# Checking equal entries in a graph kernel: a compare on the transposed blocks replaced by one on natural rows that TensorE adds up

## The chip, the cores and the metric

The kernel runs on one core of a Trainium2 chip. The time is the device time of one launch in microseconds (us), as the median of several runs on the same chip. The engines are TensorE (PE in the profile), VectorE (DVE), ScalarE (ACT), GpSimd (POOL) and SyncE (SP), which here issues most of the transfers. Each engine works through its own instructions in order and waits for the others by semaphores. Data lies in DRAM, in SBUF, and in PSUM, which has eight banks and takes TensorE's sums.

## The reference, cut to what matters

There are 2708 nodes with 128 features each (`x`) and an adjacency matrix `adj` of 2708 x 2708 floats. The matrix is sparse; every row has its diagonal set and is divided by its number of entries, so all nonzero entries of row i are equal to 1/degree(i).

```python
# adj: random pattern OR identity, then each row divided by its sum
# layer 0
XW = mobius_matvec(W, X)
gamma = 2.0 / jnp.maximum(1.0 - sq, EPS)               # sq = row sums of XW * XW
nominator = A_hat @ (gamma * XW)
denominator = _clamp_abs(A_hat @ (gamma - 1.0))
m = mobius_scalar_mul(0.5, nominator / denominator)
r = A_hat.sum(-1, keepdims=True)
AXW = mobius_scalar_mul(r, m)
x = _layernorm(x + expmap0(relu(logmap0(AXW))))
# layer 1
s = x @ msg_w[:, :D].T ;  d = x @ msg_w[:, D:].T
messages = gelu(s[:, None, :] + d[None, :, :] + msg_b)   # for every pair i, j
aggregated = jnp.einsum('ijd,ij->id', messages, adj)
new_feats = concat([x, aggregated]) @ upd_w.T + upd_b
x = _layernorm(x + layernorm(gelu(new_feats) + x))
```

## The kernel before, in words

**Sparsity and its check.** The kernel does not multiply by the values of `adj`, but by its pattern, and it evaluates messages for the entries that are set only. This holds if the nonzero entries of a row all equal the row's diagonal entry. The kernel counts the nonzero entries (`nn`) and the entries that equal the diagonal (`ne`); at the end a `verdict` (lines 1442 to 1476) compares the sums of the two and a few other conditions, and its flag decides whether a general path runs as well (`tc.If(dense > 0)`). With these inputs it does not.

**Layer 0, per block.** `adj` is handed over transposed, in 22 blocks of Q = 124 rows. A block b comes in two halves, each a load of 682 KB into one of three buffers `aT` (line 635), 124 partitions x 1364 floats. For each half ACT takes the sign (line 645) into a bf16 tile `sgn` and counts the entries by its accumulator. Then DVE compares the half with the diagonal (line 655), which a second small load `dgb` (line 631, 62 KB, the diagonal of the block on all partitions) has brought:

```python
V.scalar_tensor_tensor(aT, aT, 1.0, diagonal broadcast to [Q, HALF, Q],
                       op0=OP.mult, op1=OP.is_equal, accum_out=ne[:, at : at + 1])
```

The buffer is held by the load, the sign and the compare. TensorE multiplies `sgn` with `ym`, the features in three bf16 limbs and some columns of powers of two (line 670). DVE adds the limbs up (`total`, line 700) and reads from the further columns, in digits, which neighbours a row has (lines 720 and 722); ACT takes the squares and the relu.

**From sums to messages.** `batch` turns the digits of some blocks into neighbour lists: index lists `J`, and one-hot matrices `R` (line 903), for tiles of up to 128 edges. One of its steps multiplies on TensorE into a PSUM bank `sel` (line 916), and DVE finds the place of each edge in it (`nearest`, lines 921 to 931). `epilogue` does the rest of layer 0 for a chunk of blocks (0-4, 5-8, 9-13, 14-18, 19-21). `project` then stores one row of message terms per node in a table in DRAM (line 1136): table 0 for blocks 0 to 8, table 1 for blocks 9 to 21 (`CUT` = 9). `messages` works on groups of up to four tiles: POOL gathers the rows of the neighbours from a table (line 359, one gather per tile, five buffers `dd` of four tiles), TensorE spreads the terms of the receiving node (`X`, line 1189) and transposes `R` into the PSUM bank `rt` (line 1192), ACT copies that out (`turned`, line 1196), DVE adds (line 1200), ACT takes the gelu (line 1204), and TensorE collects the sums (lines 1211 to 1214). 66 tiles need table 0 only, the other 41 need table 1. `ended` and `finish` make the outputs, 22 stores.

**The order of the work.** All of it is written down as steps with a cost, the buffers that they hold (`Slot`, with the counts in `ROOM`) and a rank. A list scheduler, `Plan.order`, simulates the engines with these costs: whatever can start first is issued, and the rank decides among steps that could start within 0.04 us. So the program of each engine, SP's queue included, is a fixed order. The steps of layer 0 have the block's number as their rank, the compares b + 0.6, an epilogue the number of its chunk's end less `AHEAD`, the messages ranks from 23 (table 0) and from 40 (table 1), and the verdict 29.

Of the kernel before, what the change touches and what calls it, by code (L numbers as in the profile page):

```python
# [10 lines left out]
F32 = mybir.dt.float32  # L11
U32 = mybir.dt.uint32
BF16 = mybir.dt.bfloat16
I32 = mybir.dt.int32
AF = mybir.ActivationFunctionType
OP = mybir.AluOpType
AX = mybir.AxisListType

P = 128
Q = 124  # L20
NB = 22
NP = NB * Q
HALF = NB // 2
# [12 lines left out]
CUT = 9  # L36
# [13 lines left out]
BEHIND = 8.0  # L50
AHEAD = 1.0
SPARE = [("R", 44), ("R", 85), ("sl", 22), ("sl", 44)]
LIFT = (0.0, 0.0, 20.0, 20.0, 0.0)
PACES = (23.0, 0.1), (40.0, 0.4)
BEGUN = dict(PE=0.9, ACT=3.5, DVE=0.9, POOL=20.0, SP=3.0)
LANDED = (1.8, 3.8, 5.8, 7.8)
ENGINES = {getattr(mybir.EngineType, e) for e in ("PE", "DVE", "Activation", "Pool", "SP")}
ROOM = dict(
    op=2, sel=1, X=3, Xm=2, rt=1, ag=1, aT=3, dgb=2, sgn=2, v=2, front=1, back=2, cols=1,
    x1T=2, d=2, stmp=2, st=5, near=1, r0=2, dd=DDS, rw=2, ge=2, agT=4, fin=3,  # L60
)
ENDS = [4, 4, 4, 3, 3, 2, 1, 1]
LATE_ORDER = [9, 10, 11, 12, 13, 14, 15, 16, 17, 18, 8, 7, 0, 6, 5, 1, 4, 19, 3, 20, 2, 21]


# [92 lines left out]
def hyperbolic_then_message_kernel(  # L158
# [8 lines left out]
    adj_t: bass.AP,  # L167
    adj_r: bass.AP,
    w0: bass.AP,
# [9 lines left out]
    nc = tc.nc  # L179
    N, D = x.shape  # L180
# [44 lines left out]
    rowvec = dict(mbr=weights[:, 4 * D : 5 * D], ub=weights[:, 5 * D :])  # L225
    keep_c = const.tile([P, 2 * D + 1 + NB], F32, name="keep_c")
    nc.scalar.dma_start(keep_c, c_l)
    rowvec["lw"], rowvec["lb"] = keep_c[:, :D], keep_c[:, D : 2 * D]
    mb, dg = keep_c[:, 2 * D : 2 * D + 1], keep_c[:Q, 2 * D + 1 :]

# [10 lines left out]
    ones = const.tile([P, P], F32, name="ones")  # L241
    nc.gpsimd.memset(ones, 1.0)

    def power(o, v, k):
# [4 lines left out]
    for c in range(NB):  # L249
# [8 lines left out]
        compare_op=OP.is_equal,  # L258
# [39 lines left out]
    nn = const.tile([Q, 2 * NB], F32, name="nn")  # L298
    ne = const.tile([Q, 2 * NB], F32, name="ne")
    mv = const.tile([Q, NB, 2], F32, name="mv")  # L300
# [37 lines left out]

    def bank(name, bufs=2):
        return ps.tile([P, 512], F32, name=name, bufs=bufs)  # L340

    nc.gpsimd.memset(bias, 0.0)
# [278 lines left out]
    def layer0(b):  # L621

        dgs, ops = Slot("dgb"), Slot("op")
        home = SPARE[b - 2] if 2 <= b < 2 + len(SPARE) else None
        sgs = [] if home else [Slot("sgn")]
        st = {}
        rank = float(b)

        def diagonal():
            st["dgb"] = dgb = stream.tile([P, Q], F32, name="dgb", bufs=2)  # L630
            nc.sync.dma_start(dgb, bass.AP(tensor=adj_r.tensor, offset=adj_r.offset + b * Q, ap=[[0, P], [1, Q]]))

# [18 lines left out]

        def compare(h):
            aT = st[h][:Q]
            at = 2 * b + h
            V.scalar_tensor_tensor(  # L655
                aT,
                aT,
                1.0,
                st["dgb"][:Q].unsqueeze(1).to_broadcast([Q, HALF, Q]),
                op0=OP.mult,  # L660
                op1=OP.is_equal,
                accum_out=ne[:, at : at + 1],
            )

        def product(j0, j1):
# [7 lines left out]

        ld = add("SP", 0.38, diagonal, holds=[dgs], rank=rank, kb=62.0)
        p = None
        for h in range(2):
            ats = Slot("aT")
            la = add("SP", 0.46, lambda h=h: load(h), holds=[ats], rank=rank + 0.1 * h, kb=682.0)
            g = add("ACT", 1.33, lambda h=h: sign(h), after=[la], holds=[ats, *sgs], rank=rank)
            compared.append(add("DVE", 1.5, lambda h=h: compare(h), after=[g, ld], holds=[ats, dgs], rank=rank + 0.6))  # L680
            for j in (0, 6):
                j0, j1 = h * HALF + j, h * HALF + (6 if j == 0 else HALF)
                p = add(
                    "PE",
                    0.218 * (j1 - j0),
                    lambda j0=j0, j1=j1: product(j0, j1),
                    after=[g, p, limbed[(j1 - 1) // 4]],
                    holds=[*sgs, ops],
                    rank=rank + 0.5,
                )  # L690
# [46 lines left out]
        if not S:  # L737
            found[b] = counted[b]
        squared[b] = add("ACT", 1.08, squares, after=[summed[b]], rank=rank + 0.7)

    def batch(blocks, S, rank):
# [176 lines left out]
        def nearest(k, part, s):  # L918
            w, ta = len(part), part[0][0]
            dist = row.tile([P, 512], F32, name="dist", bufs=1)[:, : w * C].rearrange("p (t c) -> p t c", c=C)  # L920
            V.tensor_tensor(  # L921
                dist, s["sp"], place[:, ta : ta + w].unsqueeze(2).to_broadcast([P, w, C]), op=OP.subtract
            )
            yield
            near = row.tile([P, 64], F32, name="near", bufs=1)[:, :w]
            V.tensor_reduce(near, dist, axis=AX.X, op=OP.min, apply_absolute_value=True)
            yield
            if k == 0:
                V.tensor_scalar_min(J[:, ta : ta + w], near, lim[0] - 1.0)
            else:  # L930
                V.tensor_scalar(J[:, ta : ta + w], near, -float(lim[0]), lim[1] - 1.0, op0=OP.add, op1=OP.min)

        for k in range(2):
            every = []
            late = rank + 0.5 + k * BEHIND
            for i in range(n):
# [9 lines left out]
                for t in range(t0, t0 + nt):  # L946
                    hot[t] = oh
                    every.append((t, i))
            for g in range(0, len(every), 512 // C):
                part = every[g : g + 512 // C]  # L950
                w = len(part)
# [216 lines left out]
    def messages(k, blocks, rank, pace, ended):  # L1168
# [15 lines left out]
        def spread(st, group):  # L1184
            st["X"] = X = bank("X", ROOM["X"])
            st["RT"] = RT = ps.tile([P, 4, P], BF16, name="rt", bufs=1)
            for i, (t, b, *_) in enumerate(group):
# [6 lines left out]
        def turned(st, w):  # L1194
            st["rw"] = rw = edge.tile([P, 4, Q], F32, name="rw")
            A.copy(rw[:, :w, :], st["RT"][:, :w, :Q])  # L1196

# [180 lines left out]
    for b in range(NB):  # L1378
        layer0(b)
    for blocks, S in BATCHES:  # L1380
        batch(blocks, S, blocks[-1] + 1.5)
    for b0, b1 in CHUNKS:
        epilogue(b0, b1, b1 - AHEAD)

# [62 lines left out]
    def verdict2():  # L1447
# [6 lines left out]
        V.tensor_reduce(cn[:, 1:2], nn, axis=AX.X, op=OP.add)  # L1454
        V.tensor_reduce(cn[:, 2:3], ne, axis=AX.X, op=OP.add)
        V.tensor_reduce(cn[:, 3:4], deg, axis=AX.X, op=OP.add)
# [9 lines left out]
    def verdict5():  # L1466
        tot, bad = vd["tot"], vd["bad"]
        pads = float(NP - N)
        V.tensor_scalar(bad[:, 1:2], tot[:, 0:1], pads, None, op0=OP.not_equal)
        V.tensor_scalar_add(tot[:, 2:3], tot[:, 2:3], -pads * NP)  # L1470
        V.tensor_tensor(bad[:, 2:3], tot[:, 2:3], tot[:, 1:2], op=OP.not_equal)
# [92 lines left out]
def layouts(x, adj, msg_w, msg_b, upd_w, upd_b, ln_w, ln_b):  # L1564
# [10 lines left out]
    diagonal = np.zeros((P, NB), adj.dtype)  # L1575
    diagonal[:Q] = np.diagonal(whole).reshape(NB, Q).T
    return {
        "x_p": x_p,
        "x_t": xs.T,
        "w_l": np.concatenate([msg_w, upd_w, *(np.tile(v, (P, 1)) for v in (msg_b, upd_b))], axis=1),  # L1580
        "c_l": np.concatenate([*(np.tile(v, (P, 1)) for v in (ln_w, ln_b)), msg_b[:, None], diagonal], axis=1),
        "adj_t": adj_t,
        "adj_r": np.diagonal(whole).reshape(NB, Q),
    }
# [37 lines left out]
```

## Time and profile before

| What | Value |
|---|---|
| median of three runs | 371.06 us (369.29 to 371.99) |
| the profiled execution | 424.92 us |
| span of the profile | 422.8 us |
| mean granted TensorE clock in it | 0.808 |
| busy: PE / DVE / ACT / POOL | 270.7 / 282.2 / 236.4 / 166.3 us |
| 44 loads of `aT` | 682 KB each |
| 22 loads of `dgb`, 22 stores to the tables | 62 KB each |
| all DMA | 45.86 MB |
| first gather / last store of table 1 issued | 179.8 us / 313.2 us after the start of the span |

The profile is one execution, slower than the runs. Its page lists for each line of the kernel the operation, the tiles (output <- inputs), their shape, the number of instructions and their summed and mean time, and last how long the engine had been idle before them and what ended most of that. The table of windows gives for stretches of the span the busy time of the engines, in the order PE, weight loads of PE, DVE, ACT, POOL, with the number of instructions in brackets, and then the mean clock, the share of DMA and its GB/s. The chain that ended last runs back from the last instruction, at each step to whatever released it; "issue" is time in which the engine waited for nothing that the profile shows.

### The profile page before, as it was taken

Reading aid. Unit: us, or ns where it says so; the run is one execution under the profiler, and the core shown is the slowest. Engines: PE = TensorE matmul, PEld = TensorE weight load, DVE = VectorE, ACT = ScalarE, POOL = GpSimd, SP = SyncE. Lnnn points to the kernel's source line nnn. Section 1 sums busy time; section 2 is a strip of 40 time slices with the busy share of each in tenths; the row PEclk is TensorE's granted clock in tenths of the full one; section 3 lists DMA queues with packets and bytes.
Section 4 is the critical chain, followed back from the end, with each engine's and each line's share of the span. In section 5 each row is a group of like instructions: output and inputs, shape, how many; then the busy total and the mean of one; then the engine's idle time right before and its main releaser. Section 6 shows DMA issues by size and latency. Waiting matters only on the chain.

```text
span 422.8 us, 6335 instructions
## 1 busy us (share of the span) xinstructions
PE 270.7 (64%) x1769; PEld 193.0 (46%) x1769; DVE 282.2 (67%) x1224; ACT 236.4 (56%) x660; POOL 166.3 (39%) x298
## 2 busy tenths in 40 slices
PE   5300957999763888966877379854863388575720
PEld 5200534665421446644634146553653278564610
DVE  1888967799978999964986079843632028944580
ACT  2858846358885389682667076952651146543430
POOL 9940000010300001076567606782537522877240
PEclk9855698999896999997889569975997589856565
DMA  8678376207340474844247502220112200222110
GB/s 317 233 224 249 125 221 206 71 2 211 110 118 9 139 224 143 271 119 119 21 140 237 126 0 85 66 55 25 29 42 51 48 20 6 54 72 67 32 36 14
DMA packets 19601, 45.86 MB, mean 108 GB/s; under 512 B 5881, under 2 KB 11573, under 8 KB 19557
## 3 DMA queue, kind: packets, MB, share of 16 engines
q1 hardware_dynamic: 15701, 37.75, 29.4%
q0 software_dynamic: 3424, 7.02, 6.9%
q10 hardware_dynamic: 432, 0.60, 0.4%
q8 instruction: 16, 0.26, 0.3%
q14 instruction: 28, 0.23, 0.2%
HBM read 42.58 MB, written 2.78 MB: 107 GB/s over the span
## 4 chain that ended last, share of the span: by engine, by line
PE 25%; DVE 24%; ACT 14%; DMA 13%; another core or an unknown queue 10%; issue 9%; POOL 1%; ACTq 0%; SPq 0%; POOLq 0%; DVEq 0%
DMA aT<-in_adj_t_dram 11%; PE op L670 8%; DVE aT L655 5%; PE X L1189 3%; PE op L1214 3%; ACT sgn L645 2%; PE ag L1214 2%; ACT r L899 2%; PE X L1127 2%; ACT ge L1204 1%; DVE nom L543 1%; PE X L1408 1%; PE ag L1211 1%; PE rt L1192 1%
## 5 line engine op out<-in xcount | busy, mean ns | idle before, releaser
L359 POOL DMA_INDIRECT dd<-table_dram,J x107 | 112.6, 1052 | 53.6 <-issue 42.4
L670 PE MATMUL op<-ym,sgn 124*124 124x512 bf16 x396 | 104.8, 413 | 43.4 <-DVE ym L559 24.5
L670 PEld LDWEIGHTS <-sgn 124*124 124x124 bf16 x396 | 55.0, 147 | 74.1 <-DVE ym L559 24.8
L655 DVE SCALAR_TENSOR_TENSOR aT<-aT,dgb 124x1364 f32<-124x1364 f32 x44 | 69.0, 1572 | 8.7 <-ACT sgn L645 4.1
L645 ACT ACTIVATE sgn<-aT 124x1364 bf16<-124x1364 uint32 x36 | 48.2, 1340 | 12.9 <-DMA aT<-in_adj_t_dram 12.8
L979 POOL TENSOR_TENSOR knr<-knr,halves 124x10 f32<-124x10 f32 (+2 forms) x5 | 9.0, 1810 | 84.4 <-DVE knr L983 84.4
L1189 PE MATMUL X<-sl,R 124*128 124x128 bf16 x321 | 36.1, 251 | 6.7 <-issue 5.6
L1200 DVE TENSOR_TENSOR dd<-X,dd 128x512 f32<-128x512 f32 (+2 forms) x28 | 18.5, 660 | 31.7 <-remote 19.6
L1189 PEld LDWEIGHTS <-R 124*128 124x128 bf16 x321 | 29.0, 115 | 18.1 <-issue 17.0
L246 POOL TENSOR_TENSOR krs<-krs,halves 124x5 f32<-124x5 f32 (+2 forms) x5 | 5.5, 1094 | 79.6 <-DVE krs L1068 74.3
L1192 PE MATMUL rt<-identb,R 124*128 124x124 bf16 x107 | 26.7, 250 | 6.8 <-ACT rw L1196 6.6
L1204 ACT ACTIVATE ge<-dd 128x512 f32<-128x512 f32 (+2 forms) x28 | 17.2, 614 | 16.3 <-remote 6.2
L1214 PE MATMUL ag<-rw,ge 128*128 128x124 f32 x132 | 24.7, 319 | 2.3 <-ACT ge L1204 1.7
L1127 PE MATMUL X<-wall,x1T 128*124 128x512 f32 x38 | 21.4, 644 | 7.5 <-ACT x1T L1123 5.1
L921 DVE TENSOR_TENSOR dist<-sel,place 128x440 f32<-128x440 f32 (+11 forms) x17 | 6.4, 379 | 28.2 <-remote 26.1
L899 ACT ACTIVATE r<-iota,mid 124x256 f32<-124x256 f32 (+4 forms) x48 | 24.6, 534 | 0.4
L246 POOL TENSOR_TENSOR rs<-rs,halves 124x4 f32<-124x4 f32 (+3 forms) x16 | 13.6, 855 | 27.7 <-DVE rs L1270 23.7
L1214 PEld LDWEIGHTS ag<-rw,ge 128*128 128x128 f32 x132 | 21.7, 232 | 3.4 <-ACT ge L1204 2.0
L1211 PE MATMUL ag<-ident,gd 124*128 124x124 f32 x44 | 11.6, 351 | 18.1 <-issue 14.0
L705 ACT COPY cnt<-op 124x1 f32<-124x1 f32 x22 | 3.4, 153 | 32.9 <-remote 18.1
L1214 PE MATMUL op<-rw,ge 128*128 128x124 f32 x82 | 18.6, 359 | 4.9 <-ACT ge L1204 3.7
L1386 ACT COPY gd<-ag 128x124 f32<-128x124 f32 x22 | 5.8, 264 | 26.5 <-remote 21.5
(257 smaller groups left out, 666.5 us busy)
## 6 DMA issues: line engine op xcount, KB each, us to landing
aT<-in_adj_t_dram SPq DMA_DIRECT2D x44, 682.0 KB
dd<-table_dram,J POOLq DMA_INDIRECT x107
x_sb<-in_x_p_dram SPq DMA_DIRECT2D x2, 704.0 KB
own<-in_x_t_dram SPq DMA_DIRECT2D x2, 682.0 KB
dgb<-in_adj_r_dram SPq DMA_DIRECT2D x22, 62.0 KB
table_dram<-d SPq DMA_DIRECT2D x22, 62.0 KB
out_dram<-own SPq DMA_DIRECT2D x21, 62.0 KB
sl<-in_w_l_dram ACTq DMA_DIRECT2D x1, 384.0 KB
```

The costliest lines, as they stand in the source:

```text
L246: nc.gpsimd.tensor_tensor(o, v, halves[:Q, k : k + 1].to_broadcast([Q, v.shape[1]]), op=OP.pow)
L359: nc.gpsimd.indirect_dma_start(out=o, out_offset=None, in_=src, in_offset=bass.IndirectOffsetOnAxis(ap=at, axis=0))
L645: A.activation(st["sgn"][:, h * HALF : (h + 1) * HALF, :], st[h][:Q].bitcast(U32), AF.Sign, accum_out=nn[:, at : at + 1],)
L655: V.scalar_tensor_tensor(aT, aT, 1.0, st["dgb"][:Q].unsqueeze(1).to_broadcast([Q, HALF, Q]), op0=OP.mult, op1=OP.is_equal, accum_out=ne[:, ...
L670: T.matmul(op[:Q, :WIDE], lhsT=sgn[:, j, :], rhs=ym[:, j, :], start=(j == 0), stop=(j == NB - 1))
L899: A.activation(r[:, : nt * P], iota[:Q, : nt * P], AF.Abs, scale=2.0, bias=st["mid"][:, at : at + 1])
L1127: T.matmul(dp[:Q, :], lhsT=st["x1T"], rhs=wall.rearrange("p a d -> p (a d)"), start=True, stop=False)
L1189: T.matmul(X[:, i * D : (i + 1) * D], lhsT=R[:, t, :], rhs=sl[:, b, h, :], start=(h == 0), stop=(h == 2))
L1192: T.transpose(RT[:, i, :Q], R[:, t, :], identb[:Q, :Q])
L1200: V.tensor_tensor(dd, st["X"][:, : w * D], dd, op=OP.add)
L1204: A.activation(ge[:, :w, :], st["dd"][:, :w, :], AF.Gelu)
L1214: T.matmul(cur[b][:, :Q], lhsT=st["ge"][:, i, :], rhs=st["rw"][:, i, :], start=False, stop=is_last)
```

## The change

The compares on `aT` and the loads of the diagonal are taken out. `aT` is held by the load and the sign only. In their place `adj` is loaded a second time, as it lies: 22 strips of 128 rows (the last one overlaps the one before), each in two loads of 1354 columns, into the same three buffers `aT`. Here the diagonal entry belongs to the partition, so a `tensor_scalar` with a scalar per partition (`straight`) does the compare; it has no accumulator and writes ones and zeros in place. TensorE multiplies the upper 16 bits of these floats, read as bf16, by a column of ones (`picks`, for the last strip ones for the new rows only) and sums over all strips in one PSUM row, `tally`, which the verdict then adds up. In the plan the strips have the ranks 18, 19, and so on (`NAT`).

`tally` needs a PSUM bank. `sel` and `rt`, which had one each, share one now: `sel` is 256 columns wide instead of 512, so the groups of `nearest` are smaller (25 instead of 17), and `rt` is the other half and no tile of its own. `AHEAD` goes from 1.0 to 8.0 for the chunks of table 0 and to 4.0 for the others.

In the order that results, SP issues 33 loads of `aT` before the ninth store to table 0 (37 before). 18 of the 44 new loads stand before the last store to table 1, and 26 behind it. The outputs' stores come after those, the last 17 behind the load of the flag.

```diff
-AHEAD = 1.0
+AHEAD = 8.0, 4.0
+SEL = 256
+NAT = 18.0, 1.0
 ROOM = dict(
-    op=2, sel=1, X=3, Xm=2, rt=1, ag=1, aT=3, dgb=2, sgn=2, ...
+    op=2, sel=1, X=3, Xm=2, rt=1, ag=1, aT=3, sgn=2, ...
...
     def bank(name, bufs=2):
+        if name == "sel":
+            return halved[:, :SEL]
         return ps.tile([P, 512], F32, name=name, bufs=bufs)
+    halved = ps.tile([P, 512], F32, name="sel", bufs=1)
+    RT = halved[:, SEL:].bitcast(BF16).rearrange("p (t e) -> p t e", t=4)
+    tally = ps.tile([P, 512], F32, name="tally", bufs=1)[:1]
...
-        def diagonal():
-            st["dgb"] = dgb = stream.tile([P, Q], F32, name="dgb", bufs=2)
-            nc.sync.dma_start(dgb, ...)
-        def compare(h):
-            ...
-        ld = add("SP", 0.38, diagonal, holds=[dgs], rank=rank, kb=62.0)
-            compared.append(add("DVE", 1.5, lambda h=h: compare(h), after=[g, ld], holds=[ats, dgs], rank=rank + 0.6))
...
+    def equals(k):
+        rank = NAT[0] + NAT[1] * k
+        for h in range(2):
+            st, ats = {}, Slot("aT")
+            def load(st=st, h=h):
+                tile_ = stream.tile([P, HALF, Q], F32, name="aT", bufs=3).rearrange("p j q -> p (j q)")
+                st["a"] = tile_[:, :half]
+                nc.sync.dma_start(st["a"], adj[first[k] : first[k] + P, h * half : (h + 1) * half])
+            def equal(st=st):
+                V.tensor_scalar(st["a"], st["a"], straight[:, k : k + 1], None, op0=OP.is_equal)
+            def add_up(st=st, h=h):
+                high = st["a"].bitcast(BF16).rearrange("p (n two) -> p n two", two=2)[:, :, 1]
+                pick = picks[:, int(k == len(first) - 1) :][:, :1]
+                for c in range(0, half, 512):
+                    w = min(512, half - c)
+                    T.matmul(tally[:, :w], lhsT=pick, rhs=high[:, c : c + w], start=..., stop=...)
+            la = add("SP", 0.46, load, holds=[ats], rank=rank, kb=693.0)
+            eq = add("DVE", 0.09 + dve(half, 2), equal, after=[la], holds=[ats], rank=rank)
+            compared.append(add("PE", 0.75, add_up, after=[eq, *compared[-1:]], holds=[ats], rank=rank))
...
-            for g in range(0, len(every), 512 // C):
-                part = every[g : g + 512 // C]
+            for g in range(0, len(every), SEL // C):
+                part = every[g : g + SEL // C]
...
-            st["RT"] = RT = ps.tile([P, 4, P], BF16, name="rt", bufs=1)
...
+    for k in range(len(first)):
+        equals(k)
...
-        epilogue(b0, b1, b1 - AHEAD)
+        epilogue(b0, b1, b1 - AHEAD[b1 > CUT])
...
-        V.tensor_reduce(cn[:, 2:3], ne, axis=AX.X, op=OP.add)
+        V.memset(cn[:, 2:3], 0.0)
+        V.tensor_reduce(cn[:1, 2:3], tally, axis=AX.X, op=OP.add)
```

## The prediction

> **What bounds the kernel now.** I read the page's busy times first, then the table of windows, then the chain that ended last, then the queue of SP and the timeline of POOL. The page:
>
> ```profile
> PE 270.7 (64%) x1769; PEld 193.0 (46%) x1769; DVE 282.2 (67%) x1224; ACT 236.4 (56%) x660; POOL 166.3 (39%) x298
> L655 DVE SCALAR_TENSOR_TENSOR aT<-aT,dgb 124x1364 f32<-124x1364 f32 x44 | 69.0, 1572 | 8.7 <-ACT sgn L645 4.1
> ```
>
> No engine is full over the span, so the question is where one is. Windows, cut at 57 (first block sum), 108 (sum of block 8), 180 (first gather), 270 (last block sum) and 314 (last table store); the last is 314 to 423:
>
> ```profile
> 57.00:108.00 51.00, 42.55 (x218) 26.17 (x218) 42.83 (x230) 30.17 (x83) 2.57 (x2) 0.97 0.47 144
> 108.00:180.00 72.00, 55.32 (x344) 32.94 (x343) 65.73 (x284) 51.18 (x152) 6.28 (x8) 0.93 0.47 141
> 180.00:270.00 90.00, 64.81 (x413) 42.22 (x412) 60.69 (x258) 55.81 (x166) 55.28 (x47) 0.83 0.38 103
> 314.00:423.00 109.00, 58.82 (x439) 53.14 (x438) 49.91 (x235) 37.92 (x108) 53.60 (x57) 0.68 0.16 40
> ```
>
> The third busy number is DVE: 84% in 57 to 108 and 91% in 108 to 180, nobody else above 83%. The compares (line 655 alone) take 18.97, 12.67, 20.39 and 17.33 us of the first four stretches (0 to 57, 57 to 108, 108 to 180, 180 to 270), and nothing later. The chain shows the second thing they do:
>
> ```profile
> 93.65 1.50 DVE aT L655 x2
> 95.17 4.04 DMA aT<-in_adj_t_dram
> 99.24 1.44 ACT sgn L645 x2
> ...
> 164.94 1.49 DVE aT L655 x2
> 166.83 5.10 DMA aT<-in_adj_t_dram
> ...
> 174.63 1.55 DVE aT L655 x2
> 176.20 5.27 DMA aT<-in_adj_t_dram
> ```
>
> A compare ends late, only then is one of three aT buffers free, and a load of 5 us starts that ACT then waits for. So the first 270 us hang on DVE twice: by its work and by the buffers it holds. Then the gathers, and the tail behind the second table:
>
> ```profile
> 179.81 1.23 POOL L359 DMA_INDIRECT dd<-table_dram,J  x1 [13.14 <-issue]
> 262.81 50.59 SPq L1136 DMA_DIRECT2D table_dram<-d  x8
> ```
>
> The 41 late gathers can't start before the last of these stores (313.2). From there to the end it is 110 us, with DVE 46% busy and DMA at 40 GB/s.
>
> **The profiled execution against the median.** It took 424.9 us (span 422.8), the median of the runs is 371.1, 54 us less. The chain has 10% (42 us) of "another core or an unknown queue", all of it after 194 us and within bursts of gathers, when nothing but POOL moves. I read these as absent or short in the other runs; that isn't shown. Savings before 194 us I carry to the median one to one.
>
> **What the Trainium skill says.** *VectorE: DVE Perf Modes*, "The perf-mode tier table": fp32 tensor_scalar within SBUF runs at 2x (1227 ns for 2048 elements), two-tensor operations on fp32 at 1x. The trace agrees: the compare needs 1.57 us for 1364 elements, while tensor_scalar at line 903 costs 298 ns at 128 and 550 ns at 512. *SBUF — State Buffer*, "Who interferes with whom": a two-port operation of DVE locks GpSimd out, and so does one with two SBUF inputs against GpSimd's reads. The trace has the second: a gather that began at 265.40 beside a compare (265.30) took 2.31 us against 0.95 for most. The new operation contends too, so nothing is gained or lost there by kind. *PSUM — Partial Sum Buffer*, "PSUM bank collisions raise a hardware error": two engines may not touch one bank at a time. In before, sel and rt have a bank each; after, they share one, so each must wait for the other's readers. No row of before shows such a wait.
>
> **The change part by part.**
>
> 1. Removed from DVE: 44 x (1.572 + 0.082 for the accumulator's read) = 72.8 us, all before 270. Also 22 diagonal loads of 62 KB on SP's queue; they hide between the large ones, nothing.
>
> 2. Added on DVE: 44 tensor_scalar of 128x1354. From line 903's slope, 0.298 + 1226 x 0.00066 = 1.10 us; from the page's price about 0.86; at worst the compare's 1.57. I take 0.95, 42 us. By the program's order the first stands after the 17th block's sum, so hardly any of it lies where DVE is full.
>
> 3. aT is free after ACT's sign instead of after the compare. In 0 to 57 ACT waits 6.8 us in four pieces for aT with the prologue's chain behind it, and two fewer signs stand ahead of it: 6 us gained. In 57 to 108, 7 blocks take 51 us, 7.3 each. Without compares a block asks of ACT 2 x 1.53 + 1.3 (squares) + 0.15 = 4.5, of PE 22 x 0.216 + 0.1 = 4.9, of DMA 1.36 MB at the 317 GB/s of the first slice = 4.3 us. I take 5.5: 13 us gained.
>
> 4. Epilogues: AHEAD gives the chunks of blocks 0 to 8 a rank 7 lower. From block 8's sum to the first gather it is 72 us now, 20 of them compares, and four round trips to aT of 5.1 to 5.6 us lie on the chain between 142 and 181. Chunk one took 43 us (82.4 to 125.7) in a full DVE; I take 45 for chunk two: 27 gained. The first gather comes at about 135, 45 us earlier.
>
> 5. From there to the last table store. In after four more loads (two blocks) are open at that point, and 18 of the 44 new loads are mixed in. From 57 to 314 ACT has 161 us of work, DVE 191, PE 190. After: ACT 161; DVE 191 - 50 (compares after 57) + 17 + 5 = 163; PE 190 + 18 x 0.57 = 200. If the last store comes 40 us earlier (at 273, with the start 6 earlier), that is 222 us with ACT 72%, DVE 73%, PE 90% busy. PE's durations are modelled and at a lowered clock, so it may do better; 52 earlier is the end of what I believe, 28 the other (PE at 85%).
>
> 6. The tail, now 100 us from the store to the last DVE and ACT work. 26 of the new loads stand behind the last table store on SP's queue, each followed by a tensor_scalar in DVE's order and three matmuls in PE's, and joins, spreads and collects of the messages stand behind those. So a late load stops both engines. The pace p: by bandwidth 693 KB at 230 to 317 GB/s is 2.2 to 3.0 us; by buffers (5.2 for a lone load + 0.95 + 0.6 + 2 of waiting in line)/3 = 2.9. I take 3.0. After the last of them the order leaves about 9 of 41 tiles, worth 28 us now. Tail = 28 + 26p = 106, +6. TensorE's part, 26 x 3 matmuls at 0.571 a load (1354 columns at 0.216 per 512) or 1.1 at the low clock, is 15 to 28 us beside 59 busy of 109: covered; without cover it is in p. The gathers' 64 KB each share the DMA engines; 40 GB/s leaves room.
>
> 7. Smaller selects (25 groups instead of 17, each three DVE operations of 0.2 to 0.4) and the shared bank: 0 to 10 us, +3. Equals lock gathers out for part of 0.95 us each, in place of compares: nothing net. The verdict moves behind all equals; eight outputs' worth of work and 17 stores on SP stand after it, so it does not end last.
>
> Sum: -40 + 6 + 3 = -31 us, that is 394 for a profiled execution and **340** for the median. In general: 26p - 109.
>
> **Rivals.** *The tail is paced by the new loads, and most of the gain goes there.* p = 3.8, because gathers, loads and both in-order engines wait on each other: -10, 361 us. For it: lone loads take 5.1 to 5.6 us in the chain, far from bandwidth. Against: they are alone there. *The same mechanism ends slower:* if the three buffers overlap hardly at all, p = 4.8 and the tail is 153 us: +16, **387** us. It decides from p = 4.2 on. For it: SP's stores and loads are one queue, and a buffer is released only by PE, which stands in its own order; against: in the first slices DMA moves 224 to 317 GB/s with the same three buffers. *No change to measure:* p near 4.2, or DVE was never needed early and the loads simply move the wait. *tensor_scalar stays at 1x:* 27 us more of DVE, two thirds in a DVE that is 46% busy: about +8 on the forecast, within its range.
>
> **How the numbers follow.** Forecast (p 2.2 to 3.5, store 28 to 52 earlier) 0.63, range 312 to 353; gain lost in the tail, 0.16; within 1%, about what a measurement of this kernel can tell from no change, 0.06; slower 0.15. The range of 8 in 10 starts at 312 (store 52 earlier, tail +0, some of the later waits gone) and reaches past the second case and the no-change case to 374. Faster 0.79, same 0.06, slower 0.15.
>
> **What would show it.** In the profile after: no line with aT and dgb; loads in the first 100 us at 3 us apart; block 8 summed near 95 and the first gather near 135; tensor_scalar on aT 0.9 to 1.0 us; the last table store near 273; then equals 3 us apart until some 30 us before the end. Wrong, if the first gather comes after 160 (DVE was not what held it), if equals in the tail are over 4 us apart, or if DVE's waits on aT's load or PE's on the equals head the list of waits.

## The result, and the profile after

| kernel | median of 20 runs | lowest to highest |
|---|---|---|
| before | 373.35 us | 367.31 to 379.01 |
| after | 367.25 us | 362.6 to 374.27 |

The two ran side by side on one chip. The ratio is 0.988, with an interval of 0.984 to 0.993; it leaves out the runs that are more than 1.5% above the fastest of their kernel. So the change makes the kernel 3 to 6 us faster. The forecast was 31.

**Two kinds of chip.** The profile of before that the prediction was worked on took 424.9 us, and this was not one odd execution. The runs below fell on five chips. On four of them the kernel before has medians of 423 to 428 us, on the fifth 373, as on the chip of the comparison. So three profiles stand in this document: after on the chip of the comparison (363.6 us), and before and after on the slower kind of chip (`e1_before_again` 421.2 us, `e5_after_again` 419.35 us as the median of its runs). Times of different chips are compared by their ratio to the kernel before on the same chip. For the changed kernel the ratio is the same on both kinds, within the intervals: 0.984 (0.973 to 0.995) on the slower one.

The page of after, the line of the engines and, from further down, that of the new operation (busy us, mean ns, then idle time just ahead of it and what ended it):

```profile
PE 274.1 (76%) x1901; PEld 179.7 (50%) x1901; DVE 261.0 (72%) x1204; ACT 235.3 (65%) x661; POOL 166.3 (46%) x300
L755 DVE TENSOR_SCALAR aT<-aT,keep_c 128x1354 f32<-128x1354 f32 x44 | 41.2, 936 | 30.9 <-DMA aT<-in_adj_dram 29.5
```

The new compare takes 0.936 us where 0.95 was assumed, and it waits 29.5 us for its loads. From here on a strip is one of the 44 new loads, 128 x 1354. The stretches of after, cut at 57 and 108 as those of before were, then at the first gather (135), the last block sum (198), the last table store (236) and the last sum of a strip (319):

```profile
57.00:108.00 51.00, 45.87 (x253) 28.01 (x251) 43.26 (x274) 40.31 (x124) 5.54 (x6) 1.00 0.43 144
108.00:135.00 27.00, 23.79 (x140) 14.01 (x139) 19.93 (x97) 25.27 (x75) 3.39 (x3) 1.00 0.58 179
135.00:198.00 63.00, 55.35 (x383) 32.57 (x381) 51.15 (x243) 49.15 (x136) 36.53 (x33) 1.00 0.77 254
198.00:236.00 38.00, 33.48 (x315) 22.40 (x314) 32.30 (x145) 29.89 (x100) 22.62 (x21) 1.00 0.67 204
236.00:319.00 83.00, 69.34 (x569) 48.01 (x568) 50.91 (x139) 30.73 (x88) 60.22 (x56) 0.94 0.83 263
319.00:362.00 43.00, 14.68 (x103) 12.84 (x101) 28.59 (x152) 14.94 (x44) 17.31 (x20) 0.70 0.16 41
```

Read the first number after the length: TensorE is busy 84 to 90% of each of these stretches up to 319, DVE never more than 85%; ACT exceeds that in 108 to 135 alone (94%). The tail is the time from the last table store to the end. In its first 83 us (236 to 319) DMA moves 263 GB/s, where in the tail of before it moved 40. The chain that ended last, there:

```profile
247.50 6.21 DMA aT<-in_adj_dram
253.74 0.94 DVE aT L755
254.72 1.29 PE tally L762 x3
...
262.69 6.50 DMA aT<-in_adj_dram
269.29 0.94 DVE aT L755
270.27 0.77 PE tally L762 x3
271.06 5.78 DMA aT<-in_adj_dram
```

In these pieces a strip's load takes about 6 us, its compare and sum 2, and then the buffer is free for the next load: the round trip that the prediction saw on the old chain has moved to the tail.

**Where the lead goes.** The two profiles of the slower chips, in us from the start. The lead is before minus after, the last column is the lead of the run without strips, `e2_no_equals` (see below), over before:

| mark | before | after | lead | forecast lead | lead without strips |
|---|---|---|---|---|---|
| sum of block 8 | 108.2 | 84.4 | 23.8 | 19 | 24.2 |
| first gather | 180.8 | 137.6 | 43.2 | 45 | 43.6 |
| last block sum | 270.0 | 211.5 | 58.5 | - | 61.3 |
| last table store | 309.9 | 270.6 | 39.3 | 40 | 55.8 |
| first gather from table 1 (the 67th) | 312.7 | 296.3 | 16.4 | 40 | 22.4 |
| last gather | 391.4 | 388.9 | 2.5 | - | 19.5 |
| end | 419.0 | 417.9 | 1.1 | 31 | 18.5 |

These are single executions. That of before was 5 us shorter than the median of its chip (421.2 against 426.1), so its pair with after ends only 1.1 us apart, where the ratio of 0.984 is worth some 7 us.

All that was forecast up to the last table store is there. Behind it the lead melts in two steps: 23 us between the last store and the first gather from table 1, and 14 us while the 41 tiles of table 1 are worked on. The first step shows in the instructions of two lines. Before, stores first, then the gathers issued up to 310 us (x66, from and to):

```profile
L1136 SPq DMA_DIRECT2D table_dram<-d x22: 241/269/465, 117.3 to 309.9; - x22
...
L359 POOL DMA_INDIRECT dd<-table_dram,J x66: 940/952/2403, 180.8 to 306.0; - x66
```

After, on the same kind of chip, and the gathers issued up to 271 us:

```profile
L1169 SPq DMA_DIRECT2D table_dram<-d x22: 241/269/363, 95.1 to 270.6; - x22
...
L380 POOL DMA_INDIRECT dd<-table_dram,J x56: 939/944/1671, 137.6 to 269.9; - x56
```

Before, all 66 gathers of table 0 are issued when the last store goes out, and the late gathers wait for that store. After, ten are still to come when it goes out, and it is no longer what the late gathers wait for. On the chip of the comparison the profile of after says the same (49 of 66 issued at its last store, 236.0; the 67th gather 24 us later).

The second step shows in the last 41 gathers, in this order: before, after, the run without strips, and `e6_ops_only`, in which a strip's load brings 2 KB only:

```profile
L359 POOL DMA_INDIRECT dd<-table_dram,J x41: 940/945/1080, 312.7 to 391.4; - x41
L380 POOL DMA_INDIRECT dd<-table_dram,J x41: 938/952/1654, 296.3 to 388.9; - x41
L380 POOL DMA_INDIRECT dd<-table_dram,J x41: 942/947/1106, 290.3 to 371.9; - x41
L380 POOL DMA_INDIRECT dd<-table_dram,J x41: 938/955/1716, 293.4 to 377.5; - x41
```

They take 78.7, 92.6, 81.6 and 84.1 us. By these marks most of the 14 us goes with the strips' loads. The first step does not: without strips it is 33 us (a lead of 55.8 down to 22.4), not 23.

### The profile page after: what moved, and what is told of

The parts are those of the page before. It is cut to its first block, busy times and chain, and to the rows that moved or that the text cites. A ratio compares the mean times of both kernels' runs of the same rounds, so it can differ in the third digit from the quotient of the medians.

```text
span 361.9 us, 6638 instructions
## 1 busy us (share of the span) xinstructions
PE 274.1 (76%) x1901; PEld 179.7 (50%) x1901; DVE 261.0 (72%) x1204; ACT 235.3 (65%) x661; POOL 166.3 (46%) x300
## 4 chain that ended last, share of the span: by engine, by line
DMA 26%; ACT 24%; PE 21%; DVE 18%; issue 6%; POOL 3%; POOLq 0%; DVEq 0%; ACTq 0%
DMA aT<-in_adj_t_dram 11%; DMA aT<-in_adj_dram 9%; ACT sgn L662 6%; DMA dd<-table_dram,J 5%; PE op L674 4%; PE tally L762 3%; PE ag L1246 2%; ACT r L932 2%; PE X L1221 2%; PE op L1246 2%; DVE aT L755 2%; ACT ym L560 2%; POOL dd L380 1%; PE X L1160 1%; DMA own<-in_x_t_dram 1%
## 5 line engine op out<-in xcount | busy, mean ns | idle before, releaser
L674 PE MATMUL op<-ym,sgn 124*124 124x512 bf16 x396 | 96.9, 388 | 22.4 <-DVE ym L580 14.5
L674 PEld LDWEIGHTS <-sgn 124*124 124x124 bf16 x396 | 50.8, 138 | 54.5 <-DVE ym L580 14.8
L755 DVE TENSOR_SCALAR aT<-aT,keep_c 128x1354 f32<-128x1354 f32 x44 | 41.2, 936 | 30.9 <-DMA aT<-in_adj_dram 29.5
L762 PE MATMUL tally<-aT,picks 128*1 128x512 bf16 x132 | 35.0, 375 | 11.8 <-DVE aT L755 11.7
L1221 PE MATMUL X<-sl,R 124*128 124x128 bf16 x321 | 27.9, 221 | 0.0
L262 POOL TENSOR_TENSOR krs<-krs,halves 124x5 f32<-124x5 f32 (+2 forms) x5 | 6.6, 1325 | 42.7 <-DVE krs L1101 27.5
L1221 PEld LDWEIGHTS <-R 124*128 124x128 bf16 x321 | 23.7, 99 | 5.1 <-issue 4.0
L1224 PE MATMUL sel<-identb,R 124*128 124x124 bf16 x107 | 23.4, 218 | 2.6 <-DVE dist L954 1.4
L932 ACT ACTIVATE r<-iota,mid 124x256 f32<-124x256 f32 (+4 forms) x48 | 24.2, 534 | 1.5 <-DVE R L936 1.4
L762 PEld LDWEIGHTS <-picks 128*1 128x1 bf16 x132 | 8.7, 82 | 25.5 <-issue 15.9
L1228 ACT CAST rw<-sel 128x496 f32<-128x496 bf16 (+2 forms) x28 | 15.4, 549 | 8.1 <-PE ag L1246 4.4
L936 DVE TENSOR_SCALAR R<-r,dflat 124x256 bf16<-124x256 f32 (+4 forms) x48 | 17.3, 372 | 2.1 <-ACT r L932 1.9
```

The source lines that it names most:

```text
L262: nc.gpsimd.tensor_tensor(o, v, halves[:Q, k : k + 1].to_broadcast([Q, v.shape[1]]), op=OP.pow)
L674: T.matmul(op[:Q, :WIDE], lhsT=sgn[:, j, :], rhs=ym[:, j, :], start=(j == 0), stop=(j == NB - 1))
L755: V.tensor_scalar(st["a"], st["a"], straight[:, k : k + 1], None, op0=OP.is_equal)
L762: T.matmul(tally[:, :w], lhsT=pick, rhs=high[:, c : c + w], start=(k == h == c == 0), stop=(k == len(first) - 1 and h == 1 and c + w == half),
L932: A.activation(r[:, : nt * P], iota[:Q, : nt * P], AF.Abs, scale=2.0, bias=st["mid"][:, at : at + 1])
L1221: T.matmul(X[:, i * D : (i + 1) * D], lhsT=R[:, t, :], rhs=sl[:, b, h, :], start=(h == 0), stop=(h == 2))
```

## The experiments

Ratios are to the kernel before on the same chip, with the interval in brackets. Most of these medians are of four or five runs; those of `e4_ahead`, `e7_loads_only`, `e10_msgs_early` and `e14_dve_sums_late` are of 20. The marks in us (stores, gathers, sums) come from one profiled execution of each kernel.

**The two kernels again.** Both unchanged, for profiles of one kind of chip.

> The kernel before, unchanged, for a profile of an execution that is not 54 us longer than the median. Theory A (only stalls after 194 us were special in the first profile): first gather still near 180 us, last table store near 270 us, some 100 us from there to the end. Theory B (the first profile was late in its first part too): first gather at 155 to 165 us, so that only 20 to 30 of the 45 us by which the changed kernel gathers earlier are the change's, and less of its gain had to be lost later.

421.18 us; first gather 180.8, last store 309.9. A third profile of before, on another of these chips:

> The kernel before, unchanged, for a profile beside these runs. First gather near 180 us and last table store near 310 us if this is a chip on which it takes 420 us; on one where it takes 371 us, first gather near 180 us too, last store at 265 to 275 us and the end 100 us later.

431.18 us; first gather 180.9, last store 316.0. The profile that the prediction used was thus typical of its kind of chip; the long pieces on the chain after 194 us are there again. Theories A and B were about a faster execution, and neither of these was one. There is no profile of the unchanged kernel before on a chip where it takes 373 us. The nearest is `e19_no_gather_before` (below), from such a chip: it sums block 8 at 109.8 us and sends the ninth table store at 176.9 us, against 108.2 and 176.1 in `e1_before_again`. So the first part is not earlier there, which speaks against B; its last store at 276.0 us is near A's 270, but without gathers.

> The changed kernel, unchanged, beside the others on one chip. Where the kernel before takes 426 us (as in the runs so far, with joins that wait 15 to 35 us for gathers that have long landed): if those waits come only when nothing but gathers moves, the changed kernel has none and takes 362 to 372 us, 13% less; if they hit it as they hit the run without strips, 400 to 415 us.

419.35 us, ratio 0.984 (0.973 to 0.995). The changed kernel is not spared on these chips: adding loads between the gathers does not keep the stalls away.

**The removal alone, and the change without what it adds.**

```diff
 e3_no_compare (from before)
-            compared.append(add("DVE", 1.5, lambda h=h: compare(h), ...))
-        ld = add("SP", 0.38, diagonal, ...)
 e2_no_equals (from after)
-    for k in range(len(first)):
-        equals(k)
```

> The kernel before without compares and without the loads of the diagonal, otherwise as it was (ranks, banks): the equality of the entries is not checked. It gives the worth of the removal alone. Theory A (DVE and the buffers that it held set the first 270 us): 330 to 345 us. Theory B (the messages and what they wait for set the time): over 360 us. With the run without the added part it also says what the new ranks and the shared bank do.

404.35 us, 0.955 (0.945 to 0.966): the removal is worth 15 to 23 us. Neither theory's number; on these chips the 40 us that the forecast drew from the early part are out of reach even with nothing put in the compares' place.

> The changed kernel without its added part: no second loads of adj, no tensor_scalar on them, no sums on TensorE, so the equality of the entries is not checked. It gives the price of the added part where it stands. Theory A (the new loads pace the tail and eat the gain): 315 to 330 us, last table store to end 95 to 110 us instead of 126. Theory B (little was gained by taking the compares out): within 10 us of the changed kernel, 357 to 367 us.

404.25 us, 0.960 (0.947 to 0.972). The strips cost the difference to 0.984, some 10 us. The tail is 146.4 us with no strip in it, against 147.3 with them. That doesn't mean that strips cost the tail nothing: without them the 67th gather comes 36 us behind the last store instead of 26, and the 41 tiles after it take 81.6 us instead of 92.6, and the two differences cancel. Stores and gathers of this run, the gathers up to 254.2 us:

```profile
L1169 SPq DMA_DIRECT2D table_dram<-d x22: 241/242/363, 94.8 to 254.1; - x22
...
L380 POOL DMA_INDIRECT dd<-table_dram,J x48: 942/947/1224, 137.2 to 253.7; - x48
```

The last store is 56 us earlier than before, and then 18 gathers of table 0 are open; the 67th comes at 290.3. The earlier the store, the larger this backlog: over the profiles of the slower chips it is 18 gathers with the store at 254 us, 15 at 258 and 264, 10 at 266 to 274, 5 to 8 at 280 to 304, and none with the store at 307 or later.

**The ranks alone.**

```diff
 e4_ahead (from before)
-AHEAD = 1.0
+AHEAD = 8.0, 4.0
 e13_after_ahead1 (from after)
-AHEAD = 8.0, 4.0
+AHEAD = 1.0, 1.0
```

> The kernel before with the changed ranks of the epilogues alone (AHEAD 8.0 and 4.0 for 1.0). Theory A (DVE is full, so an earlier rank only pushes compares and blocks back): 365 to 378 us. Theory B (the order, not DVE's load, made the first gather late): 345 to 360 us, first gather before 150 us.

431.0 us, 1.009 (1.003 to 1.015), first gather 163.5. As theory A had it: in the kernel before, an earlier first gather is paid for later.

> The changed kernel with the epilogues' ranks as in the kernel before (AHEAD 1.0 for both). The first gather comes later (145 to 155 us). Theory M (an early first gather is worth little, since its messages wait): within 5 us of the changed kernel, perhaps faster. As I forecast it (the first gather's lead goes through to the last table store): 8 to 15 us more.

414.5 us, 0.980 (0.968 to 0.993), first gather 148.5 instead of 137.6. Eleven us of the first gather's lead are the ranks' doing, and they are worth nothing at the end.

**What a strip costs: its bytes or its work.** Three kernels beside the changed kernel on one chip.

```diff
 e6_ops_only
-                nc.sync.dma_start(st["a"], adj[first[k] : first[k] + P, h * half : (h + 1) * half])
+                nc.sync.dma_start(st["a"][:, :4], adj[first[k] : first[k] + P, h * half : h * half + 4])
-                V.tensor_scalar(st["a"], st["a"], straight[:, k : k + 1], None, op0=OP.is_equal)
+                V.tensor_scalar(<1344 columns of st["a"]>, <672 columns of weights, twice>, straight[:, k : k + 1], None, op0=OP.is_equal)
 e7_loads_only
-                V.tensor_scalar(st["a"], st["a"], ...)
+                V.tensor_scalar(st["a"][:, :4], st["a"][:, :4], ...)
-                for c in range(0, half, 512):
+                for c in (0,):   # 4 columns
 e8_dve_sums
-                V.tensor_scalar(st["a"], st["a"], straight[:, k : k + 1], None, op0=OP.is_equal)
+                V.tensor_scalar(st["a"], st["a"], straight[:, k : k + 1], None, op0=OP.is_equal, op1=OP.add, accum_out=ne[:, at : at + 1])
-            compared.append(add("PE", 0.75, add_up, ...))
```

> The changed kernel with its order unchanged, but a strip's load brings 4 columns (2 KB) instead of 1354 (693 KB); DVE compares 1344 columns of a constant tile into the same buffer and TensorE adds up 1344 columns, so the equality is not checked. Theory L (the loads pace the tail by their 5 to 6 us and three buffers): 15 to 35 us less than the changed kernel. Theory P (TensorE and DVE with the strips' work are what is full): within 5 us of it.

407.94 us, 0.959 (0.948 to 0.970).

> The changed kernel with its order unchanged and full loads of the strips, but DVE compares and TensorE adds up 4 columns of each, so the equality is not checked. Theory L: within 5 us of the changed kernel, strips still 3 us apart in the tail. Theory P: 15 to 30 us less, since 41 us of DVE and 35 us of TensorE are gone.

422.0 us, 0.992 (0.988 to 0.995). So all of the strips' work without their bytes costs nothing that shows (0.959 against 0.960 with no strips), and the bytes without the work cost as much as the whole strip. Theory L is right on what of a strip costs, but its size is 2.5%. The compare in the page of the first and of the second of these kernels:

```profile
L756 DVE TENSOR_SCALAR aT<-sl,keep_c 128x1344 f32<-128x1344 f32 x44 | 39.7, 911 | 5.3 <-DMA aT<-in_adj_dram 5.1
```

```profile
L755 DVE TENSOR_SCALAR aT<-aT,keep_c 128x4 f32<-128x4 f32 x44 | 10.4, 238 | 32.5 <-DMA aT<-in_adj_dram 29.5
```

40 us of DVE in the one are hidden; 29.5 us of waiting for loads in the other are not. The likely reason, which isn't shown, is that joins and finishing steps stand behind the waiting compare in DVE's order. The bytes show in the 41 tiles of table 1: they take 95.9 us with the loads alone and 84.1 with the work alone.

> The changed kernel with the strips' sums taken by the tensor_scalar's own accumulator instead of TensorE: 132 matmuls (35 us) less, and what the accumulator costs on DVE; the sums are not compared with the count. If the accumulator form keeps 0.94 us, theory P gives 8 to 20 us less than the changed kernel and theory L 0 to 5 less (a buffer comes free 0.7 us sooner). If it costs the 1.57 us of the old compare, DVE gets 28 us more: 0 to 10 us more than the changed kernel.

413.8 us, 0.973 (0.962 to 0.983); beside the changed kernel 5.5 us less by the medians, intervals overlapping. The accumulator form costs the old compare's price:

```profile
L757 DVE TENSOR_SCALAR_CACHE_REDUCE aT<-aT,keep_c 128x1354 f32<-128x1354 f32 x44 | 70.8, 1613 | 5.4 <-DMA aT<-in_adj_dram 2.7
```

1.613 us plus 0.082 for reading the accumulator, so DVE has 33 us more (44 x (1.613 + 0.082 - 0.936)), and the kernel is not slower for it. The expectation tied such a price to a loss, and that was wrong. This run changes two things at once: DVE's added work may be covered where the strips stand, as `e6_ops_only` has it, or made up for by the 132 matmuls that TensorE no longer has. The Trainium skill has this difference (*SBUF — State Buffer*, "Who interferes with whom": tensor_scalar can use both ports, but not the form that also writes out its accumulator); the runs put 0.936 against 1.613 us to it.

**Where strips and messages stand.**

```diff
 e9_strips_late          -NAT = 18.0, 1.0   +NAT = 30.0, 1.0
 e12_strips_early        -NAT = 18.0, 1.0   +NAT = 6.0, 0.8
 e10_msgs_early          -PACES = (23.0, 0.1), (40.0, 0.4)   +PACES = (12.0, 0.5), (40.0, 0.4)
```

> The changed kernel with the strips ranked from 30 instead of 18 (NAT): 33 of the 44 loads stand behind the last table store instead of 26, mixed with the second table's messages and the outputs. Theory L (strips in the tail block the in-order engines, each by what its load is late): 7 more at 3 to 4 us each, less what the messages gain, 5 to 20 us more than the changed kernel. Theory M (the messages set the tail, strips only fill gaps, so those that come later cost less): 0 to 8 us less.

412.79 us, 0.977 (0.968 to 0.985). Faster, not slower, beside the kernel before: theory L's number falls. The last store comes at 257.8, 13 us earlier than in the changed kernel's profile.

> The changed kernel with the strips ranked 6, 6.8, 7.6 and so on, among the blocks of layer 0: all 44 loads stand before the last table store. Theory L: the tail loses its strips, 5 to 15 us less than the changed kernel. Theory M: layer 0, whose buffers and TensorE (88% busy between 108 and 234 us) the strips now share, takes 44 times 1.5 to 3 us less what was idle, and the messages come no sooner: 10 to 40 us more.

433.08 us, 1.019 (1.003 to 1.036), slower. With all strips ahead of the last store the tail is down to 111.5 us, but the last store goes back to 319: theory M.

> The changed kernel with the messages from table 0 ranked from 12, by 0.5 a group, instead of from 23 by 0.1. Theory M (the 66 tiles of table 0 wait for layer 0 on TensorE and DVE and then hold up the other 41): their gathers end sooner and the whole takes 5 to 15 us less than the changed kernel. Theory L: no change beyond 3 us.

Inconclusive in its time: the median is 421.96 us beside 422.9 for before, and there is no ratio with an interval. Its profile (420.42 us), set beside that of `e5_after_again`, shows what is traded. 12 of the 28 joins stand before the last block sum, not 3, and the 67th gather comes 10 us behind the last store, not 26; but the last block sum is at 261.3 us instead of 211.5, and the last store at 295.2 instead of 270.6. Messages that move forward push layer 0 back.

Set side by side, the last table store is at 258, 271 and 280 us in `e9_strips_late`, `e5_after_again` and `e13_after_ahead1`, and the ends at 410, 418 and 410 (single executions, on two chips): the end does not follow the store.

**Is TensorE the limit?** TensorE is busy 84 to 90% in the windows above, so it was the first suspect for the backlog.

```diff
 e15_pe_half_after, e16_pe_half_before
-                T.matmul(op[:Q, :WIDE], lhsT=sgn[:, j, :], rhs=ym[:, j, :], start=(j == 0), stop=(j == NB - 1))
+                c = 0 if j in (0, NB - 1) else 256
+                T.matmul(op[:Q, c:WIDE], lhsT=sgn[:, j, :], rhs=ym[:, j, c:], start=(j == 0), stop=(j == NB - 1))
```

> The changed kernel with less work for TensorE and nothing else changed: in 20 of the 22 products of a block only columns 256 to 511 are summed, so the values (not the neighbour lists) are incomplete. It takes some 440 x 0.108 = 47 us off TensorE, 28 of them after 108 us. Theory P (after the first gather TensorE is what layer 0, strips and messages share, so moving one forward pushes another back): 15 to 35 us less than the changed kernel. Theory W (what the in-order engines wait for, loads and gathers, sets that part): 0 to 8 us less.

417.46 us, 0.979 (0.969 to 0.989). TensorE's busy time falls from 296 us in `e5_after_again` to 261, and the kernel from 0.984 to 0.979, with overlapping intervals.

> The same cut of TensorE's columns in the kernel before. If DVE and the buffers that it held set its first 270 us, as forecast, the cut is worth little there: 0 to 10 us less than the kernel before. If it is worth as much as in the changed kernel (15 to 35), TensorE was a bound before as well, and taking work off DVE could not bring the 40 us.

419.85 us, 0.982 (0.973 to 0.991), 4 to 12 us. Theory P falls on these chips: 35 us less of TensorE are worth about 2 us in the changed kernel, and the 67th gather still comes 25 us behind the last store (266.4, 291.6). On a chip where before takes 373 it wasn't tried.

**Are the gathers the limit?** A memset in the place of every gather, in both kernels; these two fell on a chip where before takes 373 us.

```diff
 e18_no_gather_after, e19_no_gather_before
-            gather(st["dd"][:, i, :], tables[k], J[:, t : t + 1])
+            nc.gpsimd.memset(st["dd"][:, i, :], 0.0)
```

> The changed kernel with every gather replaced by a memset of the same 128 x 128 tile on POOL, in the same place of the order: no neighbour's row is read (the messages lack that term), and nothing waits for the tables. Theory G (gathers, their pace on POOL and what waits for them set the stretch from the first gather on, and ate the 40 us): far below the 419 us of the changed kernel, 330 to 360, and by 20 to 40 us below the kernel before without gathers. Theory E (the in-order engines' own waits do it): also faster than with gathers, but within 10 us of the kernel before without gathers.

351.94 us, 0.941 (0.934 to 0.947).

> The kernel before with the same memsets in place of its gathers. Theory G: 360 to 385 us, since DVE and its buffers still hold up the first 270 us, 20 to 40 us more than the changed kernel without gathers. Theory E: within 10 us of that one.

358.58 us, 0.960 (0.953 to 0.967). Without gathers either kernel is 15 us shorter (373.25 to 358.58; after, from the 367.25 of the comparison, 351.94), and the change is worth 6.6 us, as with them: theory E. Last store and joins (first and last) in before without gathers, then in after without gathers:

```profile
L1136 SPq DMA_DIRECT2D table_dram<-d x22: 241/269/460, 119.3 to 276.0; - x22
L1200 DVE TENSOR_TENSOR dd<-X,dd x28: 284/684/693, 189.0 to 337.8; 128x512 f32<-128x512 f32 x26, 128x256 f32<-128x256 f32 x1, 128x128 f32<-128x128 f32 x1
```

```profile
L1169 SPq DMA_DIRECT2D table_dram<-d x22: 241/273/368, 94.6 to 236.4; - x22
L1232 DVE TENSOR_TENSOR dd<-X,dd x28: 278/684/692, 141.9 to 330.0; 128x512 f32<-128x512 f32 x26, 128x256 f32<-128x256 f32 x1, 128x128 f32<-128x128 f32 x1
```

The last store is 39.6 us earlier, the last join 7.8. Between them, the last join of table 0 (the 17th of 28) is at 285.4 and 264.2, a lead of 21, and from the first to the last of table 1's 11 joins it is 50 and 59 us. It is the same pattern as with gathers: 18 us lost from the store to the end of table 0's messages, 13 in table 1's.

**Two of the edits together.** DVE's sums with the strips ranked from 30.

> The two edits that were faster than the changed kernel together: sums by DVE's accumulator (1.1% faster beside it) and strips ranked from 30 (0.8%); the sums are not compared with the count. Theory P: 400 to 412 us where the kernel before takes 425, 2 to 4% faster than the changed kernel. If DVE's slower form stands in the way of the outputs at the end: no faster than the changed kernel.

422.29 us, 0.988 (0.985 to 0.992): no gain over the changed kernel. `e9_strips_late` and `e13_after_ahead1`, which keep the whole check, came out at 0.977 and 0.980; their intervals overlap the changed kernel's, so neither is shown to beat it.

## Why the prediction was wrong, step by step

The direction was right, the size was not: 31 us forecast, 6 measured.

- **Steps 1 to 3, right, a little low.** 44 compares are gone, 44 operations of 0.94 us have come. Block 8 is summed 24 us earlier (19 forecast, which is 89 us; the list of signs says 95, and the steps don't give that). The removal does free buffers and DVE: in `e3_no_compare` alone block 8 is summed at 89.7 us.
- **Step 4, right in its number, wrong in its worth.** The first gather comes 43 us earlier (45 forecast; at 135.0 us on the chip of the comparison, as written). Part of it is the ranks', and a lead there is not a lead of the kernel: moving it by 11 us (`e13_after_ahead1`) did nothing to the end.
- **Step 5, right.** The last table store comes 39.3 us earlier, 40 forecast. The count of open loads was off (by the trace of before 35 loads of `aT`, not 37, stand ahead of the ninth store, so two more are open then, not four), without harm to the number. But it was the wrong mark: of 56 us of lead without strips 18 are left at the end, and of 39 with them 1 in this pair of profiles and some 7 by the ratio.
- **Step 6, the step that failed**: "Tail = 28 + 26p = 106, +6". The tail is 38 us longer (147.3 against 109.1), not 6. The sum starts the tail at the last store, because before the late gathers start there. After, they start 26 us behind it: 23 us that the sum has no term for, and that are there without strips too (33 us). Then the 41 tiles take 92.6 us instead of 78.7, 14 us. That is the term that the forecast had, with +6; some 11 of the 14 go with the strips (81.6 us without them). Its picture of them was wrong in part: the pace p came out at 3.2 (strips from 236 to 318.6 us, 26 of them) on the chip of the comparison and at 3.9 in `e5_after_again`, with 34 to 36 us from the last strip to the last DVE and ACT work instead of 28. But p isn't set by the loads' bytes: with loads of 2 KB it is 3.6.
- **Step 7, small.** The shared bank does make waits: in the list of `e5_after_again` TensorE's transposes wait 7.8 us for DVE's reads of `sel`, in that of after 1.4. `e3_no_compare`, with the old banks and ranks, and `e2_no_equals`, with the new ones, come out at 0.955 and 0.960 with overlapping intervals, so bank and ranks together have no cost that shows.
- **The signs.** Two of the three signs of being wrong did not come: the first gather is at 135 to 138 us, and the strips are 3.2 to 3.9 us apart. The third did in part: the wait for the strips' loads heads DVE's waits in after (29.5 us). None of them looked at the 66 gathers ahead of the late ones.
- **The rivals.** "The tail is paced by the new loads, and most of the gain goes there" gave 361 us, near the 367 measured, but by luck: it took p at 3.8, where that chip showed 3.2, and its mechanism is worth only some 10 us. The larger part had no rival: that the message work, much of which before lay beside the slow first 270 us, would be in the way once these were short. The joins that start before the last block sum, before (270.0 us) and after (211.5 us):

```profile
L1200 DVE TENSOR_TENSOR dd<-X,dd x8: 672/692/693, 190.7 to 264.1; 128x512 f32<-128x512 f32 x8
L1232 DVE TENSOR_TENSOR dd<-X,dd x3: 682/690/692, 147.3 to 206.4; 128x512 f32<-128x512 f32 x3
```

  Of 28 joins 20 are still to come before, 25 after and 25 without strips. An estimate of what five joins more are worth: before, the 41 tiles take 78.7 us, 7.7 us for a group of four, so 38 us. From the last block sum to the end it is 149 us before and 192 without strips, 43 more.
- **Profile against median.** The 54 us between them were taken for absent stalls, and the gain as equal in both. The ratio is the same on both kinds of chip within the intervals, so no cost of this shows.

What holds the messages back after layer 0 has been narrowed, not settled. It isn't the strips (the 36 us lag without them), and not the new ranks or the shared bank alone (`e3_no_compare` has neither, and still ten gathers of table 0 are open at its last store and the 67th comes 18 us behind it). It isn't TensorE's amount of layer 0's work (`e15_pe_half_after`, on a slower chip), and not the gathers (`e18_no_gather_after`, on a faster one). What is left, by elimination and not by an experiment, is the waits of the in-order engines on each other, in an order planned from costs. A plan made from measured waits wasn't tried, nor was less work for ACT.

## What to carry to other kernels

When an edit frees the engine that is full, list what was running beside it for free: that work doesn't shrink with the stretch that hid it, and it can become what the end waits for when the stretch gets shorter. Before taking an event as the start of a tail, check that all that must be done by then will still be done when the event comes 40 us sooner (here: 66 gathers issued before, 56 after). A milestone's lead proves nothing until an experiment that moves the milestone alone also moves the end.

## What the runs showed of the hardware

- **Chips differ by 14% on this kernel, and the two profiles of after part behind the first gather.** The same program took 367 us on one chip and 419 on another. Up to the first gather the profiles agree within 2.6 us (block 8 at 82.7 and 84.4, first gather at 135.0 and 137.6); the last block sum is at 198.5 and 211.5, the end at 361.9 and 417.9. The granted clock is 0.92 and 0.91 up to the first gather, and 0.92 and 0.80 behind it. Stretches of 0.4 us and more between the first gather and the last instruction of the three, in which TensorE, DVE and ACT all run nothing, add up to 2.3 us on the one and 27.5 on the other. In the list of waits of the slower chip these engines wait 59 us for something that the trace does not show ("remote"); the list of the faster one has no such wait. For example, on the slower chip:

```profile
ACT gd L1420 <- remote: 15.5, 3, 6.2
ACT x1T L1156 <- remote: 12.3, 2, 8.3
DVE dd L1232 <- remote: 8.1, 1, 8.1
```

  The cause isn't known, and neither is whether the lower clock is part of it or follows from the waits. The runs without gathers fell on a chip of the faster kind, so it is open whether the difference needs gathers.
- **The accumulator takes a tensor_scalar's speed away.** 128 x 1354 floats take 0.936 us without it and 1.613 + 0.082 with it, as much as the two-tensor compare of 128 x 1364 (1.572 + 0.082).
- **Sums over partitions on TensorE.** Three matmuls with a single column of weights sum a strip of 128 x 1354, 0.375 us each on the mean over 512- and 330-column pieces: 35 us for 44 strips. Without them (`e8_dve_sums`, with DVE's accumulator in their place) the median is 5.5 us lower, with overlapping intervals.
